# Longer pauses ahead of small matmuls, statistics steps in every second round, and one more image with transposes by DMA, in a fused square-root and spectral-convolution kernel

## The chip, the cores and the metric

The kernel runs on one core of a Trainium2 chip. The metric is the device time of one execution in microseconds (us), as the median of several executions. The kernel before took 3196.84 us (three executions, 3196.34 to 3201.53). PE is the matrix engine (TensorE), DVE the vector engine, ACT the scalar engine, POOL is GpSimd, and SP is the engine that only issues DMAs (SyncE). SBUF is the on-chip memory, PSUM the memory that PE writes.

## The reference

The input x is 32 images of 32 channels of 128 × 128 float32. Two layers follow each other, each added to its input:

```python
# layer 0
x = x + _L0_conv_ref(_gn(x))     # group norm, then per channel a matrix square root:
    Y = A2 / normA ; Z = I
    for _ in range(5):           # Newton-Schulz
        T = 0.5 * (3.0 * I - Z @ Y) ; Y = Y @ T ; Z = T @ Z
    sA = Y * sqrt(normA)
# layer 1
x = x + _L1_conv_ref(_gn(x), weights1, weights2)
    # real part of a 2-D FFT, 32 x 32 modes of each of two corners mixed over channels,
    # back by the real part of an inverse FFT
```

`_gn` is a group norm over 16 groups of 2 channels, with mean and variance over a whole image's group. So layer 0 needs statistics of the input image before its first product, and layer 1 needs statistics of layer 0's output image.

## The kernel before

**Groups and lanes.** The unit of layer 0 is a group of four channels of one image: a tile of 128 × 512. 32 images of 8 groups make 256 groups. `newton` is a generator that carries one group through the square root; it yields between products. The main loop counts rounds. In each round every occupied lane (there are 9) is stepped once, and between the lanes the other queues are stepped: `prods` and `backs` at lane 0, `preps` at lane 1, `specs` at lane 2, `posts` at lane 3. All work is issued by this loop; the build then reorders instructions within an engine to a small extent, except those marked `kept`. Each engine executes its instructions in the resulting order. A `yield` in a generator therefore says how many rounds lie between two instructions, and so how much of the other work stands between them in each engine's queue.

**Two ways to transpose.** Inside `quartic` (twice per group) the matrix v must be transposed. Images for which `is_far` holds send it on a trip: VectorE transposes 32 × 32 blocks (L366), SP stores the tile to DRAM (L368) and loads it back rearranged (L376 or L379), and POOL adds r (L381). The other images transpose on PE (L306) and VectorE adds r (L275, tile w). An image with trips has a group started every 3 rounds and up to 9 lanes; one without has a group every 5 rounds and about 5 lanes. `FIRST` is the first image after those with trips; images 1 to 19 have them before. The same flag moves half of the norm of the input (tile x) from POOL (L341) to ACT (L334).

**Two stages.** While images are sent on trips the pool `early` holds extra buffers (`has_more`, up to group `MORE`). When `MORE` groups are settled, `change()` gives this memory to the tiles of layer 1's products (`diag`, `plain`). From then on `early` is None: this is the second stage. The 32 images are in three sets of 21, 8 and 3 (`GROUPS`). When a set's spectra are done, its channel mixing (`wide_products` or `small_products`, L581 and L652) and then its inverse transforms (`inverse`, L748, L770, L782, L787, L723) run among the remaining images' square roots. The inverse reads layer 0's output back from DRAM.

**The statistics.** `prep(b)` makes layer 0's constants of image b, one image ahead: eight loads and bn_stats (L195), then `moments`: the sum a_ms on VectorE (L164), a matmul with a constant matrix that sums over partitions (L167), differences, then the sum a_qs (L201), its matmul (L206), two roots, and the scales. One step is taken at lane 1 of every round. If the constants are not there when a group of the image is staged, the loop steps `prep` until they are.

**After a group.** `settle` stores the group's output to DRAM (tile mid, L421), folds its halves on POOL for the transform (tile fold, L426) and takes bn_stats (L430). After four groups `forward` multiplies two folds on PE (L447, L453, L459), copies and transposes the result. After eight groups `spectrum` runs: matmuls (L484), `moments` with tag b, the sums b_qs, b_qr and b_mr, the matmuls over them (L509, L512), a root, a transpose of z, and a store (L538).

Of the kernel before, what the change touches and what calls it, by code (L numbers as in the profile page):

```python
# [46 lines left out]
EYE = 36 / 16  # L47
QS = EYE / QD
MS = -QA * QS
FIRST = GROUPS[0] - 1  # L50
MORE = FIRST * 8 + 6
NB = 8
EPS = 1e-5
K = 64
# [12 lines left out]
def conv_preact_kernel(  # L67
# [89 lines left out]
    def moments(st, tag):  # L157

        per = st.shape[1] // G
        f = st.rearrange("p (g c) (e t) -> p g (c e) t", c=per, t=3)
        ms = small.tile([P, G], F32, tag=f"{tag}_ms", name=f"{tag}_ms")
        nc.vector.tensor_reduce(ms, f[:, :, :, 1], AX.X, ALU.add)  # L164
        yield
        pm = bank()[:, 0, 0:G]
        nc.tensor.matmul(pm, avg_mean, ms, start=True, stop=True)  # L167
        nm = small.tile([P, G], F32, tag=f"{tag}_nm", name=f"{tag}_nm", bufs=2)
        nc.vector.tensor_scalar_mul(nm, pm, 2 / per)
        d = small.tile([P, G, 2 * per], F32, tag=f"{tag}_d", name=f"{tag}_d")  # L170
        nc.vector.tensor_tensor(
            d, f[:, :, :, 1], nm[:, :, None].to_broadcast([P, G, 2 * per]), ALU.add
        )
        nc.vector.tensor_mul(d, d, d)
        nc.vector.scalar_tensor_tensor(d, d, 128.0 / per, f[:, :, :, 2], ALU.mult, ALU.add)
        return ms, nm, d

    kept = tc.keep_in_program_order

    def prep(b, made):  # L180

        st = small.tile([P, C, 6], F32, tag="a_st", name=f"a_st{b}", bufs=2)
        tiles = []

        def load(i):
            t = stp.tile([P, 4, P], F32, tag="xs", name=f"xs{b}_{i}")
            kept(nc.scalar.dma_start(out=t, in_=xt_in[b, :, 4 * i : 4 * i + 4, :]))
            tiles.append(t)

        for i in range(3):  # L190
            load(i)
        yield
        for i in range(C // 4):
            for c in range(4):
                nc.vector.bn_stats(st[:, 4 * i + c, :], tiles[i][:, c, :])  # L195
            yield
            if i + 3 < C // 4:
                load(i + 3)
        _, nm, d = yield from moments(st, "a")
        q = small.tile([P, C], F32, tag="a_qs", name=f"a_qs{b}")  # L200
        nc.vector.tensor_reduce(  # L201
            q, d.rearrange("p g (c e) -> p (g c) e", e=2), AX.X, ALU.add
        )
        yield
        pq = bank()[:, 0, 0:C]
        nc.tensor.matmul(pq, avg_mean, q, start=True, stop=True)  # L206

        v = small.tile([P, C + G], F32, tag="a_v", name=f"a_v{b}")
        nc.vector.tensor_scalar_mul(v[:, 0:C], pq, -512 / (P * P))
        yield  # L210
        vg = small.tile([P, G], F32, tag="a_vg", name=f"a_vg{b}")
        nc.vector.tensor_reduce(
            vg, v[:, 0:C].rearrange("p (g c) -> p g c", c=2), AX.X, ALU.add
        )
        nc.vector.tensor_scalar(v[:, C:], vg, 0.5, EPS, ALU.mult, ALU.add)
        s = root(v, C + G, "a_r")
        iv = small.tile([P, C + G], F32, tag="a_inv", name=f"a_inv{b}")
        nc.vector.reciprocal(iv, s)
        yield

        sc = small.tile([P, C], F32, tag="a_sc", name=f"a_sc{b}", bufs=2)
        nc.vector.tensor_scalar_mul(sc, iv[:, 0:C], MS / P)
        n = small.tile([P, G, 2], F32, tag="a_n", name=f"a_n{b}")
        nc.vector.tensor_tensor(  # L224
            n,
            s[:, 0:C].rearrange("p (g c) -> p g c", c=2),
            iv[:, C:, None].to_broadcast([P, G, 2]),
            ALU.mult,
        )
        nn = small.tile([P, C], F32, tag="a_nn", name=f"a_nn{b}")  # L230
        nc.vector.tensor_scalar_mul(
            nn, n.rearrange("p g c -> p (g c)"), P * (1.5 / EYE) ** 2
        )
        sn = root(nn, C, "a_t")

        scr = small.tile([P, C], F32, tag="a_scr", name=f"a_scr{b}", bufs=2)
        nc.vector.tensor_scalar_mul(scr, sc, QR * QS / MS)
        off = small.tile([P, G, 2], F32, tag="a_off", name=f"a_off{b}", bufs=2)
        nc.vector.tensor_tensor(
            off,  # L240
            scr.rearrange("p (g c) -> p g c", c=2),
            nm[:, :, None].to_broadcast([P, G, 2]),
            ALU.mult,
        )
        off = off.rearrange("p g c -> p (g c)")
        offm = small.tile([P, C], F32, tag="a_offm", name=f"a_offm{b}", bufs=2)
        nc.vector.tensor_scalar_mul(offm, off, MS / (QR * QS))
        made[b] = (nm, sc, offm, sn, scr, off)
        yield
# [186 lines left out]
    def forward(b, q, u):  # L436


        fs = [folds.pop((b, 2 * q + i)) for i in range(2)]
        ps = bank()  # L440
        out = ps.rearrange("p j x -> p (j x)").rearrange("p (c h) -> p c h", h=64)
        cos, sin = (slice(T_FW.start + 32 * i, T_FW.start + 32 * i + 32) for i in range(2))

        for i in (1, 0):
            rows = slice(64 * i + 32, 64 * i + 64)
            kept(
                nc.tensor.matmul(  # L447
                    out[rows, :, 1:64], tab[:, sin], fs[i][:, :, 65:128], start=True, stop=True
                )
            )  # L450
            rows = slice(64 * i, 64 * i + 32)
            kept(
                nc.tensor.matmul(out[rows], tab[:, cos], fs[i][:, :, 0:64], start=True, stop=True)  # L453
            )

        for i in (1, 0):
            rows = slice(64 * i + 32, 64 * i + 64)
            kept(
                nc.tensor.matmul(  # L459
                    out[rows, :, 0], tab[:, cos], fs[i][:, :, 64], start=True, stop=True  # L460
                )
            )
        sw = sp.tile([P, 4, P], F32, tag="sp", name="sw", bufs=2)
        nc.scalar.copy(sw, ps)
        yield
        ps = transposed(sw)
        for i in range(2):
            c = 8 * q + 4 * i
            nc.scalar.copy(
                u[:, :, :, c : c + 4].rearrange("h s l c -> h (s l) c"),  # L470
                ps[:, :, 64 * i : 64 * i + 64].rearrange("h c m -> h m c"),
            )
        yield

    def spectrum(b, u, st):
# [28 lines left out]
        nc.vector.tensor_copy(qr, q[:, None, :].to_broadcast([P, 8, G]))  # L504
        mr = small.tile([P, 2, G], F32, tag="b_mr", name=f"b_mr{b}")
        nc.vector.tensor_copy(mr, ms[:, None, :].to_broadcast([P, 2, G]))
        yield
        pv = bank()[:, 0, :]
        nc.tensor.matmul(  # L509
            pv[:, 0:1], qr.rearrange("p l g -> p (l g)"), avg_v, start=True, stop=True  # L510
# [365 lines left out]
    while todo or any(lanes) or posts or specs or prods or backs:  # L876
        tail = not todo and not any(lanes)
        if early and len(settled) >= MORE:
            change()
        if tail and not posts and not late:  # L880

            phase.close()
            late.append(ctx.enter_context(tc.tile_pool(name="late", bufs=1)))
            for kk in range(2, KK):
                late_wts.append(late[0].tile([P, 2, 4, 4, C], F32, name=f"wt{kk}_late"))
                nc.gpsimd.dma_start(out=late_wts[-1], in_=wk[kk])
        for i in range(LANES):
            step(norms)
            far = todo and is_far(todo[0][0])
            under_way = [is_far(lane[0]) for lane in lanes if lane]  # L890
            room = far or under_way.count(False) + 0.6 * under_way.count(True) < LESS
            if lanes[i] is None and todo and room and rounds >= due:
                due = max(due, rounds - 1) + (FAR if far else NEAR)
                while norms:
                    step(norms)
                b, g = todo.pop(0)
                xt = ready[0][0]
                lanes[i] = (b, g, xt, newton(g, made[b][3], *ready.pop(0), far, has_more(b, g)))
                if stages:
                    stage()  # L900
            if lanes[i] is not None:
                b, g, xt, steps = lanes[i]
                if next(steps, lanes) is lanes:
                    lanes[i] = None
                    end(b, g, xt)
            if i == 1:
                step(preps)
            if i == 2 or tail:
                step(specs)
            if i == 3 or tail:  # L910
                step(posts)
            if i == 0 and rounds % 3 or tail:
                step(prods)
            if i == 0 and (rounds % 3 == 0 or holding) or tail and not (posts or specs):
                step(backs)
        rounds += 1
# [64 lines left out]
```

## Time and profile before

| | |
|---|---|
| median of three executions | 3196.84 us |
| the profiled execution | 3206.91 us, its span 3205.1 us |
| busy: PE, DVE, ACT, POOL | 2973.7, 2316.5, 1701.5, 2003.6 us |
| mean granted clock of PE | 0.965 |
| DMA | 637.55 MB, mean 199 GB/s |

The profile is one execution. "Busy" is time in which an engine executes; a wait is idle time just before an instruction, listed with what ended it. `PE ps L206 <- DVE a_qs L201: 16.0, 9, 2.6` reads: matmuls of line 206 that write tile ps waited for VectorE's a_qs of line 201, 16.0 us in total, 9 times, the longest 2.6 us. In lines of the timeline the first number is the start in us from the span's start, the second the length; a wait stands in brackets at the end. A float32 product of 128 × 128 by 128 × 128 leaves two matmul records, so a block of four products is x8. PEclk is the share of its full clock that PE was granted.

### The profile page before, as it was taken

The numbers are of one execution on the slowest core, as the hardware profiler recorded it, in microseconds if no ns is written. First come the engines' busy times: TensorE is split into PE (matmuls) and PEld (weight loads), VectorE is DVE, ScalarE is ACT, GpSimd is POOL, SyncE is SP. The second block draws the span as 40 slices with busy tenths as digits, with TensorE's granted clock in tenths as the row PEclk, the third lists the DMA queues.
The fourth block names the chain that finished last, engine by engine and source line by source line (L and its number), as shares of the span: only waits on it lengthen the run. The fifth ranks groups of instructions, "written<-read, shape, count | busy, mean of one in ns | idle before, by whom it ended". The sixth has DMA issues, their size and how long they took to land.

```text
span 3205.1 us, 78907 instructions
## 1 busy us (share of the span) xinstructions
PE 2973.7 (93%) x29440; PEld 2850.6 (89%) x29440; DVE 2316.5 (72%) x5158; ACT 1701.5 (53%) x4148; POOL 2003.6 (63%) x2314
## 2 busy tenths in 40 slices
PE   6999999999999999999999999999999898999964
PEld 6899989999999999999999998889888888998953
DVE  5777777778778877788777765677776776756645
ACT  3555556565556555656655454455455454536533
POOL 3566666667667766667666443476767666646742
PEclk9999999999999999999999999999999999999975
DMA  3566666666666666666665346766676566476577
GB/s 126 164 204 193 202 187 199 208 202 212 199 200 213 196 201 190 202 201 208 211 198 159 96 148 206 221 219 216 214 232 219 194 231 206 160 224 212 187 264 232
DMA packets 482317, 637.55 MB, mean 199 GB/s; under 512 B 97936, under 2 KB 263056, under 8 KB 481936
## 3 DMA queue, kind: packets, MB, share of 16 engines
q1 hardware_dynamic: 366592, 413.82, 40.6%
q10 hardware_dynamic: 113328, 211.34, 21.2%
q0 software_dynamic: 2016, 7.34, 0.6%
q8 instruction: 235, 3.85, 0.5%
q14 instruction: 146, 1.20, 0.1%
HBM read 398.75 MB, written 233.57 MB: 197 GB/s over the span
## 4 chain that ended last, share of the span: by engine, by line
PE 68%; DVE 12%; DMA 11%; issue 3%; POOL 3%; ACT 2%; SPq 1%; ACTq 0%; DVEq 0%; POOLq 0%
PE ps L300 55%; PE ps L306 6%; DMA xs<-in_xt 4%; DMA w<-turn 2%; DVE turn L366 2%; PE ps L770 2%; PE ps L447 1%; DVE v L275 1%; DVE a_st L195 1%; POOL yt L723 1%; DVE q L275 1%; DMA yt<-mid 1%; PE ps L748 1%; DVE yt L787 1%; PE ps L581 1%
## 5 line engine op out<-in xcount | busy, mean ns | idle before, releaser
L381 POOL TENSOR_TENSOR w<-w,r 128x512 f32<-128x512 f32 x304 | 386.5, 1275 | 352.0 <-DMA w<-turn 300.9
L300 PE MATMUL ps<-w,v 128*128 128x128 f32 x4096 | 556.2, 280 | 8.9 <-POOL w L381 3.6
L334 ACT ACTIVATE b<-b,a_off,a_scr 128x128 f32<-128x128 f32 x1024 | 470.1, 490 | 144.5 <-issue 48.6
L300 PE MATMUL ps<-y,q 128*128 128x128 f32 x4096 | 531.2, 278 | 11.8 <-ACT d L782 9.9
L300 PEld LDWEIGHTS ps<-w,v 128*128 128x128 f32 x4096 | 506.2, 195 | 13.3 <-POOL w L381 5.8
L300 PEld LDWEIGHTS ps<-y,q 128*128 128x128 f32 x4096 | 496.6, 195 | 16.0 <-ACT d L782 10.4
L426 POOL TENSOR_TENSOR fold<-xt 128x256 f32<-128x256 f32 x512 | 363.6, 730 | 217.7 <-DVE xt L413 194.4
L275 DVE SCALAR_TENSOR_TENSOR q<-ps,eye 128x512 f32<-128x512 f32 x512 | 349.2, 682 | 174.4 <-PE ps L300 168.6
L723 POOL TENSOR_TENSOR yt<-yt,d 128x512 f32<-128x512 f32 x238 | 299.9, 1287 | 177.6 <-ACT d L782 132.2
L341 POOL TENSOR_SCALAR x<-xt,a_nm,a_sc 128x128 f32<-128x128 f32 x720 | 315.5, 450 | 20.4 <-DVE a_n L224 20.4
L409 ACT ACTIVATE y<-ps,a_t_s 128x128 f32<-128x128 f32 x1024 | 291.3, 368 | 63.6 <-PE ps L300 63.1
L195 DVE BATCH_NORM_STATS2 a_st<-xs 128x6 f32<-128x128 f32 x1024 | 227.2, 279 | 134.3 <-DMA xs<-in_xt 133.7
L294 POOL TENSOR_TENSOR r<-mb,eye 128x512 f32<-128x512 f32 x104 | 132.5, 1274 | 304.4 <-ACT mb L269 298.9
L300 PE MATMUL ps<-x,b 128*128 128x128 f32 x2048 | 279.4, 280 | 5.7 <-POOL x L341 5.6
L269 ACT ACTIVATE t<-ps 128x512 f32<-128x512 f32 x256 | 152.5, 596 | 247.6 <-PE ps L300 240.6
L366 DVE STREAM_TRANSPOSE turn<-v 128x512 f32<-128x512 f32 x304 | 277.6, 913 | 5.3
L300 PE MATMUL ps<-m,q 128*128 128x128 f32 x2048 | 280.1, 281 | 0.5 <-DVE q L275 0.5
L300 PE MATMUL ps<-m,mb 128*128 128x128 f32 x2048 | 280.2, 281 | 0.1
L300 PE MATMUL ps<-y,t 128*128 128x128 f32 x2048 | 277.4, 279 | 2.7 <-ACT d L782 1.4
L300 PE MATMUL ps<-x,q 128*128 128x128 f32 x2048 | 277.8, 279 | 1.9 <-DVE q L275 1.9
L413 DVE TENSOR_TENSOR xt<-ps,xt 128x512 f32<-128x512 f32 x256 | 175.4, 685 | 143.6 <-PE ps L300 141.0
L300 PE MATMUL ps<-q,t 128*128 128x128 f32 x2048 | 275.6, 278 | 0.0
(124 smaller groups left out, 5827.2 us busy)
## 6 DMA issues: line engine op xcount, KB each, us to landing
turn<-turn SPq DMA_DIRECT2D x304, 256.0 KB
b<-in_x ACTq DMA_DIRECT2D x256, 256.0 KB
xt<-in_xt ACTq DMA_DIRECT2D x256, 256.0 KB
xs<-in_xt ACTq DMA_DIRECT2D x256, 256.0 KB
mid<-xt SPq DMA_DIRECT2D x256, 256.0 KB
yt<-mid SPq DMA_DIRECT2D x128, 512.0 KB
out<-yt SPq DMA_DIRECT2D x109, 512.0 KB
w<-turn SPq DMA_DIRECT2D x152, 256.0 KB
```

The costliest lines, as they stand in the source:

```text
L195: nc.vector.bn_stats(st[:, 4 * i + c, :], tiles[i][:, c, :])
L275: nc.vector.scalar_tensor_tensor(s, ps, f, t, ALU.mult, ALU.add)
L300: nc.tensor.matmul(ps[:, j, :], lhsT[:, j], rhs[:, j], start=True, stop=True)
L306: nc.tensor.transpose(ps[:, j, :], t[:, j, :], ident)
L334: nc.scalar.activation(t, x, AF.Identity, bias=offset[:, c], scale=scale[:, c])
L341: nc.gpsimd.tensor_scalar(m[:, j, :], xt[:, j, :], nm[:, c // 2 : c // 2 + 1], sc[:, c : c + 1], ALU.add, ALU.mult,)
L366: nc.vector.transpose(blocks(t), v.rearrange(form, b=4))
L381: nc.gpsimd.tensor_tensor(w, w, r, ALU.add)
L409: nc.scalar.mul(y[:, j, :], py[:, j, :], sn[:, c : c + 1])
L413: nc.vector.tensor_tensor(xt, products(t, y), xt, ALU.add)
L426: nc.gpsimd.tensor_tensor(f[:, :, 64 * half : 64 * half + 64], xt[:, :, 0:64], xt[:, :, 64:128], op)
L723: engine.tensor_tensor(yh, yh, d, op)
```

## The change

Four edits. `FIRST` becomes 21, so images 1 to 20 have trips, 20 instead of 19; `MORE` becomes 170 instead of 166 groups. In `moments` (for both layers), in `prep` and in `spectrum` the single yield between a small sum on VectorE and the matmul over it becomes two yields. `forward` yields once before its matmuls. In the second stage `preps` is stepped only in odd rounds.

```diff
-FIRST = GROUPS[0] - 1
-MORE = FIRST * 8 + 6
+FIRST = GROUPS[0]
+MORE = FIRST * 8 + 2
@@ moments
         nc.vector.tensor_reduce(ms, f[:, :, :, 1], AX.X, ALU.add)
-        yield
+        yield from pause
         pm = bank()[:, 0, 0:G]
@@
+    pause = (None, None)
@@ prep
             q, d.rearrange("p g (c e) -> p (g c) e", e=2), AX.X, ALU.add
         )
-        yield
+        yield from pause
         pq = bank()[:, 0, 0:C]
@@ forward
+        yield
         fs = [folds.pop((b, 2 * q + i)) for i in range(2)]
@@ spectrum
         nc.vector.tensor_copy(mr, ms[:, None, :].to_broadcast([P, 2, G]))
-        yield
+        yield from pause
         pv = bank()[:, 0, :]
@@ main loop
-            if i == 1:
+            if i == 1 and (early or rounds % 2):
                 step(preps)
```

In the built program of the changed kernel 64 transposes on PE (of v, L306), 16 additions on VectorE (w) and 16 norms on POOL are gone, and 16 block transposes on VectorE, 16 additions on POOL (w), 16 norms on ACT, and 16 stores and 40 loads on SP are added. Two of the inverse's additions and one output store stand on other engines (DVE and ACT) than before.

## The prediction

> **What bounds the kernel now.** I read the page first (shares, slices), then the waits of TensorE by stage, then single stretches of the timeline. PE is 93% busy over the span and above 95% in most of the first stage, so its idle time is what can be won, and its own work is the floor.
>
> ```profile
> PE 2973.7 (93%) x29440; PEld 2850.6 (89%) x29440; DVE 2316.5 (72%) x5158; ACT 1701.5 (53%) x4148; POOL 2003.6 (63%) x2314
> PEclk9999999999999999999999999999999999999975
> ```
>
> The stages by window (columns: length, busy time of PE, PEld, DVE, ACT, POOL with counts, granted clock, DMA share, GB/s): the stage of trips, about 100 to 1720 us; the stage without, about 1900 to 3080. After 3080 is the tail, at clock 0.58.
>
> ```profile
> 100.00:1720.00 1620.00, 1565.95 (x13876) 1518.43 (x13869) 1278.69 (x2885) 949.34 (x2346) 1095.49 (x1213) 0.98 0.65 201
> 1900.00:3080.00 1180.00, 1108.45 (x12034) 1048.40 (x12033) 791.75 (x1714) 592.13 (x1430) 734.08 (x873) 0.98 0.65 212
> ```
>
> What PE waited for between 100 and 1720 us (total, times, longest). Nearly everything is one kind: a matmul over a small sum (L206, L509) that stands in PE's queue before VectorE has made the sum. The names b_r_q and b_inv mean that VectorE was late with its queue.
>
> ```profile
> PE ps L206 <- DVE a_qs L201: 16.0, 9, 2.6
> PE ps L509 <- DVE b_qr L504: 8.1, 4, 2.7
> PE ps L206 <- DVE b_r_q L150: 7.1, 2, 3.7
> PE ps L206 <- DVE b_inv L521: 5.2, 2, 3.2
> PE ps L206 <- DVE b_r_q L152: 4.4, 2, 2.5
> PE ps L300 <- POOL w L381: 3.6, 2, 2.2
> ```
>
> The same between 1900 and 3080 us; L447, the forward transform, waits for POOL's folds.
>
> ```profile
> PE ps L206 <- DVE a_qs L201: 17.9, 6, 8.9
> PE ps L447 <- POOL fold L426: 12.0, 6, 4.4
> PE ps L300 <- ACT d L782: 11.3, 4, 4.5
> PE ps L509 <- DVE b_qr L504: 6.7, 3, 3.1
> ```
>
> A wait costs more than its length. After the 3.73 us wait at 1649, eight matmul records take 2.06 us instead of 1.06; in a window around another such wait the clock is 0.57, and 1.00 on either side.
>
> ```profile
> 1649.02 0.61 PE L206 MATMUL ps<-a_qs,avg_mean 128*128 128x32 f32 x2 [3.73 <-DVE b_r_q L150]
> 1649.44 2.06 PE L300 MATMUL ps<-x,q 128*128 128x128 f32 x8
> ...
> 1654.01 1.06 PE L300 MATMUL ps<-m,q 128*128 128x128 f32 x8
> ```
>
> ```profile
> 174.00:178.00 4.00, 3.84 (x20) 3.81 (x21) 1.99 (x9) 0.32 (x2) 0.42 (x2) 0.57 0.51 162
> 178.00:188.00 10.00, 10.00 (x92) 10.00 (x92) 9.47 (x31) 5.50 (x14) 5.17 (x7) 1.00 0.63 195
> ```
>
> The clock record holds 14 half-speed stretches between 100 and 1720 us, of 3.41 or 6.83 us; 13 begin around an L206 or L509 wait of 1.9 us or more, one after the POOL wait.
>
> **What the Trainium skill says.** "TensorE: Matmul & The Clock Gate", Part 1 (The HAM clock gate): the clock is halved when PE has been idle for a window of about 3.4 us, and busy time lifts it. The trace agrees on the half clock and the 3.41 us; it differs on the cause, since waits of 1.93 us were enough. The same page, Part 2 (step 1): matmuls stay in program order, only weight loads are pulled ahead; so everything behind L206 waits with it, as the trace shows. "SBUF — State Buffer" (its terms): VectorE and GpSimd take a shared port pair exclusively. The trace fits: in the 8.86 us wait at 2514, VectorE's a_d of 64 columns took 6.87 us (2506.1 to 2512.9) under an almost unbroken run of POOL additions, against 0.74 us on average.
>
> **The change part by part.**
>
> *Pauses of two rounds before the sums' matmuls (L167, L206, L509), and in the second stage a statistics step only every second round.* No work is added. I measured in the built instruction order how much PE work (a block of four products 0.89 us, of four transposes 0.44) stands between the last PE result that VectorE must take before the sum and L206. Before: 0.2 to 3.9 us. Changed: 2.9 to 8.1 in the first stage, 8.6 to 15.6 in the second. Old room plus old wait gives the need: at most 5.6 us in the first stage, 10 for the 8.86 us wait. For L509 the room goes from 0.2–6.1 to 2.9–14. So L206 is covered nearly everywhere, L509 mostly. The cover is other images' products on PE; where it fails, the wait returns at 1 to 2 us. What VectorE queues behind L169 and L209 may now wait for PE instead; it is 79% busy there and has that time. Late next would be the statistics: their last root still stands 35 to 55 ACT instructions ahead of first use (before 92 to 113), so no image starves.
>
> First stage: waits of L206 32.7, L509 8.1, L167 1.2: 42.0 us. Half-speed stretches after them: 54.6 us in sum; less the waits inside, halved: 25.7. Together 67.7; I take 93%, 63, and give 3 back for more waiting on POOL's w, whose trip has a fixed length while the rounds get shorter: 60. From 1720 to 1900 there is one wait of 1.0: 1.
>
> Second stage, L206 17.9 whole, L509 75% of 6.7, L447 80% of 12.0: 32.5. Clock in the same shares 4.2 + 4.0 + 2.7: 10.9. Of these 43.4 I give back 13, about one more time the 11.3 us of waits on ACT's d, because DMA, ACT and POOL fill each other's gaps here: 30.
>
> *Forward one round later.* Its room after the last product of its half image goes from 4.2–9.6 us to 6–15 in the second stage; it is the 80% above. Fold buffers (3) still turn over in time: the next but one starts six rounds later.
>
> *Image 20 with trips; four more groups with the larger buffers.* It removes 16 blocks of PE transposes:
>
> ```profile
> 1888.28 0.60 PE L306 MATMUL ps<-ident,m 128*128 128x128 f32 x4
> 1888.72 1.06 PE L300 MATMUL ps<-x,q 128*128 128x128 f32 x8
> ```
>
> Four stand 0.44 us apart from the next block: 16 × 0.44 = 7.0 us of PE. It adds 16 VectorE transposes (913 ns) for 16 sums (683): 3.7 us; on POOL 16 w additions (1275), 20.4, less 16 norms (450), 7.2; on ACT 16 norms (493), 7.9; on SP 16 stores and 40 loads of about 0.4 us issue each, 22 us. All hide under PE: 1720 to 1900, where image 20 was, had DMA at 33%. In the order of SP the spectrum's store stands among trips as before. Group 0's products now follow their memsets by three groups instead of five; the last memset ended 48 us ahead of the first product before, and three fifths are 29. Worth 7, bounds 0 to 8.
>
> *Tail.* One half-step of the inverse (12 matmuls, 2 additions of 1355 ns, a 0.5 MB store) moves behind the last product: 2 us lost, between 0 and 5.
>
> Sum: 60 + 1 + 30 + 7 − 2 = 96 us, from an execution of 3206.9 us (span 3205.1), which lies 10 above the median. I take the difference off the median: 3196.8 − 96 = 3101.
>
> **Rivals.** *Second stage gives nothing* (0.17): its waits move to ACT's d and to loads, since four engines are near their limits in turn. For it: L300 waits there already; against: the largest waits are L206's, with 8 us more room. 3196.8 − 66 = 3131.
>
> *Lateness only moves* (0.06): VectorE is late anyhow, and PE meets it at the next q or v; only the transposes are saved: 3190. Against: VectorE itself waits 240 us for PE in the first stage, and other PE waits there are rare.
>
> *Slower* (0.08): POOL's wait for trips becomes the bound. In the first stage POOL works 57.7 us of an image's 85.3 and waits 15.1 for trips:
>
> ```profile
> POOL w L381 <- DMA w<-turn: 287.0, 116, 7.1
> ```
>
> If that wait grew to 27.6 us per image it would set today's pace; at 33, PE would lose 5.4 on each of 20 images, and 110 us eat all gains: 3210. For it: SP is one queue, and spectrum stores and trips shift against each other. Against: PE waited for w only 3.6 us.
>
> **Numbers.** The likeliest case (0.69) has its own range of 3075 to 3125. All waits and clock of the targeted lines gone, nothing given back: 67.7 + 1 + 36.6 + 12.6 + 7 = 125, so 3072; 3070 is the lower end. The upper end, 3147, takes in the second-stage rival with a first stage at 75%. About 0.2% (6 us) is what can be told from no change. Faster 0.90, same 0.02, slower 0.08: nearly all of the moved-lateness case counts as just faster.
>
> **What would show it.** Right: L206 and L509 under 5 us in the first stage's PE waits; clock 1.00 there; PE over 99% busy; L206 gone after 1900 and L447 under 4; 768 instead of 832 transposes of v. Wrong: new PE waits on POOL's w or VectorE's q (moved lateness, trips), half-speed stretches without such waits, L300 on ACT's d well over 25 us, or a long first L581 wait.

## The result and the profile after

| | before | after |
|---|---|---|
| median of four executions | 3196.59 us (3195.75 to 3201.53) | 3153.78 us (3144.42 to 3160.40) |
| ratio, 95% interval | | 0.9861 (0.983 to 0.9892) |
| the profiled execution, its span | 3206.91, 3205.1 us | 3144.42, 3142.4 us |
| mean granted clock of PE | 0.965 | 0.970 |

The changed kernel is 1.4% faster: 43 us, where 96 were forecast. Neither the likeliest time (3101) nor the range (3070 to 3147) held it. Lines stand two further down from L178 on and three from L442 on, so L206, L300, L306, L447, L509, L581, L652, L782 and L787 of before are L208, L302, L308, L450, L512, L584, L655, L785 and L790.

First the page after: the shares of the engines, the clock in forty slices, and the group of transposes of v.

```profile
PE 2943.9 (94%) x29376; PEld 2825.3 (90%) x29376; DVE 2318.1 (74%) x5160; ACT 1705.9 (54%) x4164; POOL 2014.8 (64%) x2312
PEclk9999999999999999999999999999999999999975
L308 PE MATMUL ps<-ident,v 128*128 128x128 f32 x768 | 117.5, 276 | 3.6 <-DVE v L277 2.2 <-DVE xt L415 1.4
```

The page hardly tells where the time went: shares move by one or two per cent, and its slices round the clock away. The stages do. In both traces I took the time at which VectorE had made the last output tile (xt) of certain images, the idle time of PE between these (waits over 0.2 us), and the clock's loss (half of the half-speed time outside the waits).

| from the end of image ... to ... | before | waits, clock | after | waits, clock | forecast |
|---|---|---|---|---|---|
| start to 1 | 246.4 | | 241.2 | | |
| 1 to 18 (trips) | 1452.5 | 45.0, 24.0 | 1398.4 | 12.9, 5.1 | −60 from the start |
| 18 to 21 (image 20 among them) | 269.5 | | 254.9 | | −8 |
| 21 to 31 (second stage) | 1113.6 | 68.9, 26.3 | 1119.5 | 67.3, 27.4 | −30 |
| tail | 123.1 | | 128.3 | | +2 |

The first stage gave 59, image 20 another 15; the second stage gave nothing, it lost 6. The next view is the table by windows of after, the stage of trips and the second stage with the same columns as before.

```profile
100.00:1660.00 1560.00, 1539.48 (x13831) 1495.54 (x13831) 1277.18 (x2877) 949.55 (x2349) 1092.56 (x1208) 0.99 0.68 209
1820.00:3014.00 1194.00, 1123.06 (x12146) 1063.30 (x12148) 794.86 (x1733) 593.75 (x1437) 736.51 (x878) 0.97 0.65 210
```

PE is busy 98.7% of the first window (96.7% before) and 94.1% of the second (93.9% before). What PE waited for in the first stage, 100 to 1720 us:

```profile
PE ps L308 <- ACT sw L467: 5.8, 6, 1.6
PE ps L302 <- POOL w L383: 4.4, 3, 3.8
PE ps L308 <- ACT m L271: 3.7, 3, 2.1
PE ps L208 <- DVE a_qs L203: 2.5, 2, 1.7
```

L208, 32.7 us before, is down to 2.5, L512 (8.1 before) does not appear, and nothing large has come instead. Now the second stage, 1895 to 3000 us:

```profile
PE ps L302 <- ACT d L785: 17.5, 6, 5.4
PE ps L655 <- DMA diag<-xs: 6.7, 1, 6.7
PE ps L584 <- DMA diag<-in_wk: 6.1, 3, 3.3
PE ps L308 <- ACT m L271: 6.0, 3, 4.0
PE ps L308 <- ACT sw L467: 5.2, 2, 3.2
PE ps L302 <- DVE q L277: 5.1, 2, 4.9
PE ps L302 <- DVE w L277: 4.6, 2, 4.1
```

Here too the targeted waits are gone: L208 on a_qs, 17.9 before, does not appear, L450 on folds went from 12.0 to 1.1. But ordinary products (L302, L308) now wait for ACT's d, m and sw and VectorE's q and w, and the sum is what it was. Behind about half of that time (33 of 67 us, counted further down) stands one thing: VectorE waiting at the head of its queue for a load of the statistics. VectorE's and ACT's waits in the second stage (1895 to 3014 and 1895 to 3000 us; before, the same groups had 54.9 in 22 times and 31.8 in 40):

```profile
DVE a_st L197 <- DMA xs<-in_xt: 81.8, 41, 8.5
```

```profile
ACT d L785 <- DVE yt L790: 59.4, 47, 9.8
```

The timeline shows how they hang together, engine by engine: first ACT (its queue, ACTq, issues the load), then VectorE, then PE.

```profile
2086.81 0.36 ACTq L189 DMA_DIRECT2D xs<-in_xt  x1
2087.75 0.67 ACT L785 COPY d<-ps 128x256 f32<-128x256 f32 x2
2094.08 0.37 ACT L785 COPY d<-ps 128x256 f32<-128x256 f32 x1 [5.66 <-DVE yt L790]
2095.06 0.60 ACT L271 ACTIVATE m<-ps 128x512 f32<-128x512 f32 x1
...
2092.58 0.87 DVE L197 BATCH_NORM_STATS2 a_st<-xs 128x6 f32<-128x128 f32 x4 [8.53 <-DMA xs<-in_xt]
2093.37 1.27 DVE L790 TENSOR_TENSOR yt<-ps,yt 128x512 f32<-128x512 f32 x2
...
2094.50 2.08 PE L302 MATMUL ps<-m,q 128*128 128x128 f32 x8 [5.43 <-ACT d L785]
```

The load of the next image's statistics was issued at 2086.8 and its data came at 2092.6. VectorE stood for 8.53 us at the statistics over it, with an addition of the inverse (yt, L790) in its queue behind. ACT's d had to wait for that yt, and behind d in ACT's queue was m, the operand of PE's next product; PE stood 5.43 us. The product's records then take 2.08 us instead of 1.06: the clock is halved again. The profile names "ACT d", but the late thing is a load two engines away.

And this load was late for a reason of its own. ACT's queue stood at it for 4.89 us, from 2081.89 to 2086.77. In the trace's semaphore records the load uses the semaphore of an output store of the inverse (out, L714), which SP had issued at 2078.07, and the wait ended as the last part of that store landed (2086.75). In the view of these semaphore waits (count; shortest, median and longest in ns; first and last start) it is the longest:

```profile
L189 ACTq EVENT_SEMAPHORE  x113: 17/17/4887, 7.6 to 2791.7; - x113
```

A second profile of after has the same wait at the same place, 4.40 us long. It is the only long one at these loads in the second stage (5.2 us in sum), so it explains the stretch shown and not the other stops.

### The profile page after: what moved, and what is told of

Same layout as the page of the kernel before. It is cut to its first block, busy times and chain, and to the rows that moved or that the text cites. A ratio compares the mean times of both kernels' runs of the same rounds, so it can differ in the third digit from the quotient of the medians.

```text
span 3142.4 us, 78894 instructions
## 1 busy us (share of the span) xinstructions
PE 2943.9 (94%) x29376; PEld 2825.3 (90%) x29376; DVE 2318.1 (74%) x5160; ACT 1705.9 (54%) x4164; POOL 2014.8 (64%) x2312
## 4 chain that ended last, share of the span: by engine, by line
PE 77%; DMA 9%; DVE 8%; ACT 2%; issue 2%; SPq 1%; POOL 1%; ACTq 0%; DVEq 0%; POOLq 0%
PE ps L302 64%; PE ps L308 7%; DMA xs<-in_xt 3%; PE ps L773 2%; PE ps L450 1%; DMA w<-turn 1%; DVE yt L790 1%; PE ps L584 1%; DMA yt<-mid 1%; DMA or<-od 1%; PE ps L751 1%; PE ps L487 1%; DMA plain<-in_wk 1%; DVE a_st L197 1%; DMA b<-in_x 1%
## 5 line engine op out<-in xcount | busy, mean ns | idle before, releaser
L383 POOL TENSOR_TENSOR w<-w,r 128x512 f32<-128x512 f32 x320 | 406.9, 1275 | 365.3 <-DMA w<-turn 290.0
L302 PE MATMUL ps<-w,v 128*128 128x128 f32 x4096 | 556.7, 280 | 14.7 <-POOL w L383 4.4
L302 PE MATMUL ps<-y,q 128*128 128x128 f32 x4096 | 532.8, 278 | 5.2 <-ACT d L785 2.1
L302 PEld LDWEIGHTS ps<-w,v 128*128 128x128 f32 x4096 | 506.4, 195 | 23.6 <-POOL w L383 5.5
L302 PEld LDWEIGHTS ps<-y,q 128*128 128x128 f32 x4096 | 495.3, 194 | 9.7 <-ACT d L785 2.8
L343 POOL TENSOR_SCALAR x<-xt,a_nm,a_sc 128x128 f32<-128x128 f32 x704 | 308.9, 450 | 19.7 <-DVE a_n L226 19.7
L296 POOL TENSOR_TENSOR r<-mb,eye 128x512 f32<-128x512 f32 x96 | 122.4, 1275 | 277.9 <-ACT mb L271 274.4
L368 DVE STREAM_TRANSPOSE turn<-v 128x512 f32<-128x512 f32 x320 | 292.0, 912 | 5.3
L302 PE MATMUL ps<-m,q 128*128 128x128 f32 x2048 | 277.9, 279 | 12.9 <-ACT d L785 8.6
L302 PE MATMUL ps<-x,b 128*128 128x128 f32 x2048 | 279.9, 281 | 5.6 <-POOL x L343 5.6
L302 PE MATMUL ps<-x,q 128*128 128x128 f32 x2048 | 277.1, 278 | 5.9 <-DVE q L277 5.9
L302 PE MATMUL ps<-y,t 128*128 128x128 f32 x2048 | 276.9, 279 | 6.1 <-ACT d L785 3.3
L302 PE MATMUL ps<-q,t 128*128 128x128 f32 x2048 | 274.0, 277 | 3.1 <-ACT gt L757 1.8
L302 PE MATMUL ps<-m,mb 128*128 128x128 f32 x2048 | 275.8, 278 | 0.7 <-DVE t L277 0.7
L302 PEld LDWEIGHTS ps<-m,q 128*128 128x128 f32 x2048 | 253.6, 195 | 16.2 <-ACT d L785 9.3
```

What stands on the lines that cost most here:

```text
L302: nc.tensor.matmul(ps[:, j, :], lhsT[:, j], rhs[:, j], start=True, stop=True)
L343: nc.gpsimd.tensor_scalar(m[:, j, :], xt[:, j, :], nm[:, c // 2 : c // 2 + 1], sc[:, c : c + 1], ALU.add, ALU.mult,)
L368: nc.vector.transpose(blocks(t), v.rearrange(form, b=4))
L383: nc.gpsimd.tensor_tensor(w, w, r, ALU.add)
```

## The experiments

Each is compared with the kernel before on the same chip. "First stage" is image 1 to 18 and "second stage" 21 to 31, from one profile of each. Single profiled executions of a kernel differ: two of after had first stages of 1398.4 and 1397.5, second stages of 1119.5 and 1119.4, and 254.9 and 263.0 between. A profiled execution can also lie well off its kernel's median: 19 us below it without the statistics loads, 13 below with pauses only, 10 above with the inverse later by one. Where in the execution such a difference lies is not known, so a difference of some 10 us between the stages of two kernels rests on one profile of each and is weak by itself.

| kernel | us | ratio | first stage | 18 to 21 | second stage |
|---|---|---|---|---|---|
| before | | | 1452.5 | 269.5 | 1113.6 |
| after, again | 3151.68 | 0.9849 (0.9826 to 0.9872) | 1397.5 | 263.0 | 1119.4 |
| steps every round | 3159.98 | 0.9869 (0.9829 to 0.991) | 1402.2 | 266.7 | 1118.9 |
| pauses only | 3150.08 | 0.9842 (0.9809 to 0.9876) | 1413.0 | 269.3 | 1084.7 |
| every second round only | 3186.35 | 0.9959 (0.9945 to 0.9973) | 1450.1 | 269.7 | 1103.3 |
| trips only | 3189.06 | 0.997 (0.9956 to 0.9984) | 1445.2 | 259.6 | 1106.1 |
| without forward's yield | 3160.53 | 0.9881 (0.9857 to 0.9904) | 1423.6 | 266.0 | 1110.5 |
| pauses and every second round | 3138.18 | 0.9798 (0.9777 to 0.982) | 1419.6 | 267.1 | 1088.2 |
| no statistics loads in stage two | 3102.80 | 0.9693 (0.9665 to 0.9721) | 1394.2 | 254.0 | 1067.6 |
| lanes in turn | 3160.40 | 0.9874 (0.985 to 0.9898) | 1402.4 | 256.8 | 1130.6 |
| lanes mixed | 3154.36 | 0.985 (0.9824 to 0.9876) | 1412.1 | 273.3 | 1097.3 |
| loads four ahead | 3173.18 | 0.9909 (0.9885 to 0.9932) | 1420.5 | 262.0 | 1119.1 |
| both of these (turn, four) | 3167.49 | 0.9898 (0.9872 to 0.9923) | 1410.8 | 261.7 | 1126.6 |
| inverse later by one step | 3117.57 | 0.9747 (0.9724 to 0.977) | 1403.7 | 256.8 | 1090.9 |
| by two | 3126.35 | 0.9775 (0.9753 to 0.9796) | 1402.4 | 256.2 | 1103.6 |
| by three | 3132.12 | 0.9784 (0.9759 to 0.981) | 1400.0 | 254.6 | 1096.0 |
| pauses, second round, later by two | 3136.07 | 0.9787 (0.9765 to 0.9808) | 1423.8 | 267.4 | 1083.3 |
| later by one, no forward's yield | 3172.06 | 0.9899 (0.988 to 0.9917) | 1423.0 | 265.3 | 1109.6 |
| later by one, steps every round | 3138.32 | 0.9785 (0.9761 to 0.9809) | 1409.4 | 265.2 | 1103.0 |

### The parts alone

The first theory was that the statistics step every second round does the harm: it spreads an image's statistics over twice the rounds. The rivals were that it is the trips or the pauses, or no part by itself. Changed with its steps in every round:

```diff
-            if i == 1 and (early or rounds % 2):
+            if i == 1:
```

> The changed kernel with a statistics step in every round of the second stage again. Theory A (statistics loads): halving spreads each image's eight loads over more rounds and so makes VectorE stop for late loads more often (81.8 us of waits for tile xs in the second stage, 54.9 before); undone, these waits fall to about 55 us and the second stage (last product of image 21 to that of image 31, 1119.5 us) gets some 15 to 30 us shorter: about 3120 to 3140. Theory B (the lateness of VectorE only surfaces elsewhere, whatever the halving does): the second stage stays within 10 us, about 3145 to 3160. First stage as in the changed kernel under both.

The kernel before with the pauses alone:

```diff
-        yield
+        yield from pause    # in moments, prep and spectrum
```

> The kernel before with only the pauses of two rounds ahead of the sums' matmuls. Both theories: the first stage gains what the changed kernel gained there, some 55 us up to image 18, from waits of L206 and L509 and the half-speed stretches behind them. Theory A: the second stage gains too, 10 to 25 us, since the loads are not spread: about 3115 to 3135. Theory B: it gains nothing: about 3140 to 3150.

The kernel before with the slower steps alone:

```diff
-            if i == 1:
+            if i == 1 and (early or rounds % 2):
```

> The kernel before with only the halved rate of statistics steps in the second stage. First stage unchanged under both theories. Theory A: the second stage gets longer, by 5 to 25 us, with more waits of VectorE for tile xs: 3200 to 3220. Theory B: the waits of L206 (16.9 us in the second stage) are covered by two rounds instead of one and surface elsewhere, within 10 us: 3187 to 3207.

The kernel before with image 20's trips alone:

```diff
-FIRST = GROUPS[0] - 1
-MORE = FIRST * 8 + 6
+FIRST = GROUPS[0]
+MORE = FIRST * 8 + 2
```

> The kernel before with only image 20 sent on trips and four more groups with the larger buffers. Both theories: 7 us of transposes on PE saved up to image 21, nothing else: 3187 to 3193, and the interval tells whether the second stage shifts with it.

What follows: the first theory fell. With steps in every round the second stage is 1118.9, as slow as in after (1119.5), and the slower steps alone gain 12.7 us. VectorE's waits for xs there fell to 67.2 us with steps in every round, without any gain. The slower steps alone came out slightly faster than either theory had it. The trips alone gain 10. The pauses alone are as fast as the whole change, and their second stage is 1084.7: a gain of the size that was forecast for it is there (29). Up to image 18 they gain 46 us and not the 55 expected. So the second stage's loss comes from parts together.

### Pairs, and what forward's yield is worth

Changed without the yield of `forward`:

```diff
     def forward(b, q, u):
-        yield
```

> The changed kernel without forward's extra yield. Alone, the pauses took 49 us off the median, the halving 13, the trips of image 20 10, together 72, where the whole change took 45. Theory F (forward one round later costs time in the second stage): without it about 3120 to 3135, the second stage (image 21 to 31) under 1100 us. Theory I (the parts fill the same hole, VectorE's stops, and do not add up): 3145 to 3160, second stage 1110 to 1125.

The kernel before with pauses and slower steps, without trips and without the yield (the diffs are above):

> The kernel before with the pauses and the halving, without trips of image 20 and without forward's yield. Theory I: no better than the pauses alone, 3143 to 3157, although the halving alone gave 13 us. Theory F: the two add up, about 3130 to 3140.

The changed kernel once more, on the same chip as these:

> The changed kernel once more, beside the others on one chip, for its time and for how far one execution's stages differ from another's: 3145 to 3160; up to image 18 within 10 us of the first profile's 1639.6, the second stage within 15 of 1119.5.

The second stage without the yield is 1110.5, 9 us shorter, but the first stage is 25 us longer. PE's waits between 150 and 1640 us in the kernel without the yield, and then in after:

```profile
PE ps L308 <- ACT sw L466: 27.4, 18, 3.8
```

```profile
PE ps L308 <- ACT sw L467: 5.7, 5, 1.6
```

In before this wait was 2.7 us in 8 times. A stretch of the timeline without the yield, PE and then ACT:

```profile
956.66 1.06 PE L302 MATMUL ps<-y,q 128*128 128x128 f32 x8
961.24 1.11 PE L308 MATMUL ps<-ident,sw 128*128 128x128 f32 x4 [3.52 <-ACT sw L466]
...
959.33 0.23 ACT L148 ACTIVATE a_t_s<-a_nn 128x32 f32<-128x32 f32 x1 [2.84 <-DVE a_nn L233]
960.62 0.56 ACT L466 COPY sw<-ps 128x512 f32<-128x512 f32 x1
```

The pauses have moved the statistics so that ACT stands at a root whose input VectorE has not made, with the copy sw of the forward transform in its queue behind, and PE's transpose waits for sw. In the kernel without the yield, such a wait of ACT at a root lies within the 6 us before 9 of the 18 waits for sw, 17.7 of the 27.4 us; what delayed the other nine was not followed. The kernel with the pauses alone has 24.5 us of them, in 18 times. So the pauses exchange a wait on VectorE's sums for one on ACT; the yield takes most of that one away. The pauses are worth 33 to 40 us in the first stage (1452.5 against 1413.0 and 1419.6) and the yield 15 to 25 more, where it was forecast to matter only for the second stage's folds.

Pauses and slower steps without trips and yield are faster than the whole change: 0.9798 against 0.9849, the intervals apart, with the second stage at 1088.2. Something that trips and yield bring costs 30 us there: 22 come with the trips (1110.5), 9 with the yield on top of them (1119.5). Each of the two theories was right for one of these kernels: the parts add up without the trips, and do not with them.

### The statistics loads of the second stage

Is it VectorE's stop at late loads that fills the second stage? In this kernel images whose statistics are made in the second stage take the tiles that earlier images have loaded; the loads are left out, all other instructions stay.

```diff
+    held = [None] * 4
         def load(i):
+            if not early:
+                tiles.append(held[i % 4])
+                return
...
             tiles.append(t)
+            held[i % 4] = t
```

> The changed kernel without the eight statistics loads of an image in the second stage: the statistics are then taken from four tiles left by an earlier image, so this part of the computation is replaced. It takes away VectorE's waits for tile xs (81 us in the second stage) and 22 MB of 646 MB of transfers. If late loads that stop VectorE's queue are what PE waits for there (33 us of 67, with some half-speed stretches), the second stage falls by 35 to 50 us, to 1070 to 1085, and the time to about 3105 to 3120. If those stops only use up slack, it falls by less than 12: above 3140.

The second stage falls by 52 us to 1067.6, the time by 49. The windows (second stage of this kernel) and what is left of PE's waits there (1895 to 2950 us):

```profile
1820.00:2954.00 1134.00, 1096.74 (x12082) 1039.49 (x12085) 771.88 (x1659) 591.98 (x1429) 733.98 (x873) 0.99 0.63 204
```

```profile
PE ps L660 <- DMA diag<-xs: 6.4, 1, 6.4
PE ps L307 <- ACT d L790: 6.2, 4, 2.8
PE ps L307 <- DVE q L282: 5.6, 3, 4.5
```

PE is busy 96.7%, and the clock is 0.99. The waits between image 21 and 31 fall from 67.3 to 35.0, the clock's loss from 27.4 to 9.5: 50 of the 52 us. L302's wait on ACT's d (here L307, L790) falls from 17.5 to 6.2. So the loads are the cause of about half of the second stage's idle time. The run takes away the stops together with 18.9 MB of traffic and the 64 issues in ACT's queue. That it is the stops is argued, from the timeline above; no run separates them.

### Lanes and deeper loads: two repairs that were none

In the second stage 5 of 9 lanes are occupied, and which ones they are decides how far apart the groups stand within a round. I took that as the thing that trips change. Lanes filled strictly in turn:

```diff
-            if lanes[i] is None and todo and room and rounds >= due:
+            n = 8 * todo[0][0] + todo[0][1] - 171 if todo else -1
+            mine = n < 0 or i == n % 5
+            if lanes[i] is None and todo and room and mine and rounds >= due:
```

> The changed kernel, but from image 21's fourth group on the groups take lanes 0, 1, 2, 3, 4 in turn, at the same rounds as before. Which lane a group takes decides where in a round its step stands among the others' steps and the side queues. In the kernels whose image 20 has no trips the lanes come in turn by themselves; with trips the last far lanes leave the order 0, 3, 1, 2, 4. Theory L (this order is what takes the second stage's gain): the second stage falls from 1119 us to 1085 to 1098, and the time to 3120 to 3133. Theory D (the trips of image 20 shift the products' and inverse's loads against the second stage): it stays at 1108 to 1122, and the time at 3145 to 3158.

The other way round, the good kernel (pauses and slower steps) with the uneven lanes that the changed kernel has (the lines around `mine` as above):

```diff
+            mine = n < 0 or i == ((3, 5, 6, 7, 8) if n < 5 else (0, 3, 1, 2, 4))[n % 5]
```

> The counter-test: pauses and halving without trips of image 20 (3138 us, second stage 1088), with the order of lanes 0, 3, 1, 2, 4 from image 22 on, at the same rounds. Theory L: the second stage rises to 1105 to 1125 and the time to 3152 to 3170. Theory D: unchanged, 3130 to 3146.

Even lanes make the changed kernel's second stage longer (1130.6), and uneven ones cost the good kernel 9 us there, not 30. So the order of lanes is not what takes the 30 us; that it takes a part is not excluded. The whole is 16 us slower than without, 6 of it between images 18 and 21, where lanes were held back for their turn.

Then the loads: four instead of three issued ahead, in the same four buffers.

```diff
-        for i in range(3):
+        for i in range(4):
             load(i)
...
-            if i + 3 < C // 4:
-                load(i + 3)
+            if i + 4 < C // 4:
+                load(i + 4)
```

> The changed kernel with the statistics' loads issued one step earlier: four ahead instead of three, in the same four buffers. If VectorE stops because the loads are issued too late, its waits for tile xs in the second stage fall from 81 us to under 45 and the time to 3125 to 3140. If ScalarE's queue now waits for the buffer to be read, or the transfers are late however early they are issued: no gain, 3145 to 3165.

> Both edits together: lanes in turn and loads four ahead. If both theories hold, the gains add up in part: 3105 to 3122. If only the lanes count: 3120 to 3135. If neither: 3145 to 3160.

VectorE's stops at xs fell only from 81.8 to 72.9 us: the median from the end of a load's issue to the first statistics went from 5.3 to 5.8 us. It was not that the loads had to wait for a buffer: in the second stage ACT's queue stood at them for 5.9 us in all, 5.4 of these at stores of the inverse. Why an issue one step earlier gained so little was not found. The second stage stayed at 1119.1. The time rose by some 20 us (0.9909 against 0.9849), and the profile has it in the first stage (1420.5 against 1397.5, PE's waits 26.8 against 16.2 us), which was not foreseen: there ACT, whose queue issues these loads, lets PE wait 8.6 us for m and 8.2 for sw (after: 3.7 and 5.7). Deeper loading with more buffers was not tried. With both edits the kernel takes 3167.49 us, and the second stage 1126.6.

### Where the first set's inverse stands

In the build's order of work I counted in which round the first set's inverse begins, against the round in which image 22 starts. That number, taken modulo 12, is 5 in the two kernels with a good second stage (1084.7, 1088.2) and 11 in after, in the kernel with steps in every round and in that with four loads ahead (1118.9 to 1119.5). So I moved the inverse alone, by one, two or three steps of its queue (three rounds each):

```diff
-        backs.append(finish(prods))
+        backs.append(finish(prods, 0 if i else 1))    # 1, 2 or 3
...
-    def finish(queue):
+    def finish(queue, more):
         while queue:
             yield
+        for _ in range(more):
+            yield
```

> The changed kernel with the inverse of the first set of images begun one step, 3 rounds, later. Counted in rounds, an image of the second stage takes 40 and an inverse 12, so the first inverse stands at a phase to the images: the round of its first half-step less the round in which image 22 starts, modulo 12. It is 2 before, 11 in the changed kernel, 8 without forward's yield, 5 in the two kernels that have pauses but no trips of image 20. Second stages measured so far: 1085 and 1088 us (1097 with mixed lanes) at phase 5, 1110 at 8, 1119 to 1131 at 11. Theory P (that phase decides how often VectorE's stops meet the inverse's copies): here it is 2; not yet seen with pauses; between 1085 and 1119. Theory T (image 20 with trips itself slows the second stage): 1110 to 1125.

> The same, two steps (6 rounds) later: phase 5. Theory P: second stage 1083 to 1100 us, time 3118 to 3135. Theory T: 1110 to 1125 us, time 3143 to 3160.

> The same, three steps (9 rounds) later: phase 8. Theory P: second stage 1103 to 1115 us, time 3135 to 3150. Theory T: 1110 to 1125 us, time 3143 to 3160.

The same edit with two steps in the good kernel, which brings it to the number 11:

> Pauses and halving without trips of image 20 (phase 5, second stage 1088 us, time 3138), with the first inverse two steps later: phase 11. Theory P: second stage 1110 to 1128 us, time 3158 to 3175. Theory T: unchanged, 1083 to 1097 us, time 3132 to 3147.

All three are faster than the changed kernel, and none moved its first stage by more than 7 us. With one step the kernel takes 3117.57 us, 2.5% less than before, the fastest of these kernels that computes the whole reference. Its second stage (windows; waits of PE 1895 to 2990; of VectorE 1895 to 3000):

```profile
1820.00:2994.00 1174.00, 1120.57 (x12218) 1059.41 (x12220) 803.49 (x1739) 598.30 (x1450) 744.06 (x886) 0.98 0.66 214
```

```profile
PE ps L302 <- ACT d L785: 11.2, 6, 5.8
PE ps L655 <- DMA diag<-xs: 6.8, 1, 6.8
PE ps L308 <- DVE v L277: 5.1, 2, 2.8
```

```profile
DVE a_st L197 <- DMA xs<-in_xt: 66.3, 37, 6.2
```

VectorE stops 66.3 us for xs instead of 81.8; PE's waits from image 21 to 31 are 49.2 instead of 67.3 us and the clock's loss 13.4 instead of 27.4: 32 us, more than the stage's 29. Of PE's waits, those that were still on when such a stop of VectorE ended, or began within 2.5 us after it, are 18.1 us here, 33.2 in after, 19.1 in before.

The sum of VectorE's stops does not tell a good second stage from a poor one. It is 66.3 us here, 68.2 with pauses and slower steps (1088.2), but also 67.2 with steps in every round (1118.9). PE's waits close to stops, counted in the same way, are 18.1, 23.3 and 29.9. What differs between these three is how much of the stops gets through to PE.

So it is shown that trips are no obstacle: with them the second stage can take 1091 us, and in the changed kernel moving one queue by three rounds decides about 30 us of it. What this does to the work around it is not shown. The rule in the form of a number modulo 12 fell: the three kernels have 2, 5 and 8 and are all good (1090.9, 1103.6 and 1096.0), but the good kernel brought to 11 stays good (1083.3), and before, with 2, is poor (1113.6), with L206's waits still in it.

### The parts again, on the repaired kernel

With the inverse one step later, is each part worth what it was forecast to be? Without the yield of `forward`, and with steps in every round (the diffs are those above):

> The changed kernel without forward's yield, its first inverse one step (3 rounds) later: that inverse then begins in the same round, 637, as in the changed kernel, at phase 11. The phase theory in its first form has fallen (phase 11 was good without the trips of image 20, phases 2, 5 and 8 all good with them). If a place in the rounds is bad with these trips (S), the second stage is 1112 to 1125 us and the time 3148 to 3168. If it is the inverse's beginning straight behind the products that is bad with these trips (R), it is 1085 to 1100 and 3120 to 3140.

> The fastest kernel so far (first inverse one step later, 3118 us, second stage 1091) with a statistics step in every round of the second stage. If the halving is worth what it gave alone, 13 us: 3125 to 3137. If it is worth nothing once the inverse stands elsewhere: 3112 to 3124, and this version is the simpler one of the two.

Without the yield the ratio is 0.9899 instead of 0.9747, 1.5% or 49 us: in the profiles 19 in the first stage, 9 between, 19 in the second stage. Removing the yield also changes when the sets' work begins (the number is 11 again), so the last 19 are not its own for sure. With steps in every round it is 0.9785, 0.4% or 12 us, as much as the slower steps gave alone (12.7), though here the intervals overlap. The same shift is not worth the same everywhere: with steps in every round it shortens the second stage by 16 us (1118.9 to 1103.0), and without the yield by nothing (1110.5 and 1109.6; ratios 0.9881 and 0.9899). The second of these lies in neither range that was expected. So the yield is worth having once the inverse stands elsewhere, the slower steps probably are, and the poor second stage of the changed kernel belongs to its parts together; what makes a place good or bad is not shown.

What stays open: which of the inverse's transfers or instructions meets the statistics loads in after and not in the kernel with one step more. One such meeting is seen, the load at 2086.8 held up by an output store: with the inverse later by one, two or three steps ACT's queue stands at these loads for 0.4 us in all. But so it does with lanes in turn, at 1130.6. The loads land late together with the inverse's own loads and stores, and VectorE's stops and the queue positions behind them move at the same time. The runs do not separate them.

## Why the prediction was right and wrong

**First stage, 60 forecast, 59 measured: right in size, half right in cause.** The waits of L206 and L509 and the half-speed stretches went as described: waits 45.0 to 12.9, clock's loss 24.0 to 5.1 between images 1 and 18, and PE is 98.7% busy. "The Trainium skill", "TensorE: Matmul & The Clock Gate", Part 1, has the clock halved after an idle window of about 3.4 us; as in before, waits of about 2 us were enough here (2.08, 2.05 and 1.71 stand at the three half-speed stretches that are left), so a small wait costs more than its length. Two of the prediction's signs were just missed: the clock is 0.99 and not 1.00, and PE not over 99% busy. But "What VectorE queues behind L169 and L209 may now wait for PE instead" was the whole account of what would be late next. Late next was ACT with sw, in most of the time behind a root of the statistics: 27.4 us without the yield. The prediction counted the yield of `forward` in the second stage only; it was needed for 15 to 25 of the 60.

**Image 20, 8 forecast: right.** 768 transposes are there. From image 18 to 21 the two profiles of after are 15 and 7 us shorter than before. Kernels with these trips take 254 to 263 us there in ten profiles and 265 to 267 in four, those without 267 to 273; the trips alone gain 10 in time (0.997, 0.9956 to 0.9984).

**Second stage, 30 forecast, −6 measured: the step that failed.** "Of these 43.4 I give back 13, about one more time the 11.3 us of waits on ACT's d." The targeted waits went nearly as forecast (L206 17.9 to nothing, L447 12.0 to 1.1, L509 6.7 to 4.6 in 1900 to 3080: 30.9 us, where 32.5 were forecast), and as much came back: waits 68.9 and 67.3, clock's loss 26.3 and 27.4. With 6 us lost instead of 43.4 won, the give-back was about 49 us and not 13. The mechanism of the give-back was named, its size was not: I sized it by the waits that PE had shown (ACT's d, 11.3 us), not by the waits one engine further back. VectorE's 54.9 us at xs and ACT's 31.8 at yt stood in the trace of before. They rose to 81.8 and 59.4. Without the statistics loads the second stage is 52 us shorter. But stops of that size need not come back as PE's waits: with the pauses alone VectorE still stops 52.3 us at xs, and the second stage gains 29. What the prediction lacked is a term for what the other parts do to the second stage. It took image 20's trips as 7 us won and the yield as a gain at L447. In the second stage the two together cost 30 us, and a shift of the first inverse by three rounds takes 29 of them back. The rival "second stage gives nothing", at 0.17, was the case; its form, waits on ACT's d and on loads, is what the trace shows. My sign for it ("well over 25 us" on ACT's d) was wrong: 17.5, since the same lateness came through m, sw, q and w too.

A gain of this size was to be had: 29 with pauses alone, 25 with pauses and slower steps, 23 against before with the inverse later. But the 29 are not the forecast's 30 come true. Without the yield the folds' wait (L447 of before, L449 here) still stands at 11.1 of 12.0 us, so 12.3 of the 43.4 (9.6 + 2.7) were not won there; of the 31.1 for L206 and L509 nearly all came, with little given back.

**Tail, −2 forecast, −5 measured.** It is 125 to 132 us in all kernels with pauses and 121 to 124 in those without.

**The sum's starting point.** The sum was made in an execution 10 us above the median, and the difference taken off the median. Between the profiled executions the gain is 62.5 us; between after's repeat, whose profile is near its median, and before it is 55.7; between the medians 43 and 48 us. So some 8 us of the stages' gain is that before was profiled in a long execution, and another 7 to 9 that the first profile of after was a short one: before had 3184.77 to 3212.14 us in 39 executions on one chip, with a median of 3199.07. A part of those 10 us may well lie in the waits that I counted as won; that is argued, not shown. The result lies 23 us above the rival's 3131, although the rival's 66 us are close to the 62.7 by which the two profiled spans differ; and the range stopped 7 us below the result.

**Slower and moved lateness** did not come: PE waited 4.4 us for POOL's w in the first stage, 3.6 before.

## What to carry to other kernels

When the waits of the bounding engine are to be removed, follow each remaining wait back through the in-order queues of the engines behind it: the time that those engines stand at the head of their own queue, here 55 us of VectorE at a load, shows what may come back, where the wait that the bounding engine shows today does not. It is no forecast: with some 68 us of such stops the second stage took 1088 us in one kernel, with 67 it took 1119 in another. A change that delays one chain moves all that is queued behind it, so look on every engine for what shares a queue with the delayed chain, and give the second one its pause too. Where several streams of work run at fixed rounds, try shifting one of them by a few rounds once the change is in: here three rounds were worth 1.0% (33 us) to the changed kernel, where the whole change had gained 1.4 to 1.5%, and nothing to the kernel without forward's yield.

## What the hardware showed that I had not expected

The second stages of the two profiles of after agree to 0.1 us (1119.5 and 1119.4), the first stages to 0.9, while PE's waits in these second stages differ (67.3 and 71.6 us) and the times of one changed kernel's executions spread over 8 to 35 us. Two profiles do not tell whether that is the rule. Where the spread arises was not found.

Small VectorE operations beside POOL's additions: in after a difference of 128 × 64 elements, which took 0.19 us at best and 0.37 in the median of 32, took 6.72 us once, under a run of POOL's additions without a gap. PE then waited 4.93 us.

```profile
2465.47 6.72 DVE L171 TENSOR_TENSOR a_d<-a_st,a_nm 128x64 f32<-128x64 f32 x1
2472.11 0.18 DVE L509 COPY b_mr<-b_ms 128x32 f32<-128x32 f32 x1
2472.97 0.68 DVE L277 SCALAR_TENSOR_TENSOR q<-ps,eye 128x512 f32<-128x512 f32 x1
...
2473.70 1.92 PE L302 MATMUL ps<-x,q 128*128 128x128 f32 x8 [4.93 <-DVE q L277]
```

POOL's operations around its end:

```profile
2470.84 1.26 POOL L296 TENSOR_TENSOR r<-mb,eye 128x512 f32<-128x512 f32 x1
2472.09 1.73 POOL L343 TENSOR_SCALAR x<-xt,a_nm,a_sc 128x128 f32<-128x128 f32 x4
```

It ended at 2472.19, 0.09 us after one of POOL's operations. That is no chance. Of the 32 such differences in after, 7 began while POOL did nothing and took 0.19 to 0.24 us. 25 began during an operation of POOL, and 21 of these ended 0.06 to 0.12 us after the end of one (in before 24 of 26). So this difference waits for POOL, as a rule for the rest of one operation (it then takes up to 1.4 us), and in the case shown through several. Why through several was not found; the small operations directly behind it took 0.18 to 0.41 us, although POOL worked on without a gap. The room of 8 to 16 us that the pauses gave the statistics' own matmuls doesn't help here, since it is q, an operand of the square root, that stands behind.
